# The four value products of a step, each at a place of its own

## The chip, the cores and the metric

The kernel runs on one core of one Trainium2 chip. The metric is the device time of one execution, in microseconds (us). Three executions of the kernel before took 1729.24, 1733.9 and 1734.99 us (median 1733.9). A fourth, recorded by the profiler, took 1729.78 us.

## The reference, cut to what matters

A gated cross-attention block is followed by a quantised feed-forward block. The change lies in the attention, whose values are these:

```
kv = cond @ Wkv + bkv                 # 4096 keys (4 x 1024), 512 -> 2 x 512 columns
k, v = kv[..keys], kv[..values]       # 16 heads of 32 columns each
v = fq_sym(v, axis=keys)              # 127 steps of the largest magnitude of a column over all keys
attn = softmax(fq_sym(q) @ fq_sym(k)^T)   # 2048 rows x 4096 keys, for each of 16 heads
attn = fq_unsigned(attn)              # 255 steps of a row's largest value
out = (attn @ v) @ Wp + bp
```

All four batches are one sequence here: 2048 query rows meet 4096 keys in each of the 16 heads. The values of a head group (four heads, 128 columns) need a scale over all 4096 keys before any of them can be rounded.

## The kernel before, in words

A first part (to about 240 us) projects queries and keys, stores the turned context rows `cT` in DRAM, and makes the values of head group 0. The attention then runs from about 240 to about 1465 us in 256 steps `i`, one for each head and each tile of 128 query rows. The feed-forward block follows.

The order of instructions on every engine is the order in which the program issues them (`manual_schedule`). A step of the attention has three chunks of keys (`CHUNKS`: 1536, 1536 and 1024 wide). For chunk `n`, `scores(i, n)` issues three, three or two matmuls into a PSUM tile `ps_s` (line 689), and then one VectorE instruction (line 698) which multiplies the scores by the keys' scales, writes them to the SBUF buffer `s` or `third`, and keeps the row maximum. There are two `ps_s` tiles, so that a chunk's matmuls wait until VectorE is done with the chunk two before.

After each chunk the loop runs what a plan holds for that place. `plan[i, n]` is a list of small pieces of work that are spread over the steps by hand: `plan[i, 0]` is run after chunk 0 of step `i`, `plan[i, 1]` after chunk 1, `plan[i, 2]` after chunk 2. Two kinds of work in it matter here.

The first is attention times values. `plan_values` puts a block of 32 small matmuls (`products(k)`, line 768) at place 1 of every step from step 8 on; ahead of it GpSimd casts the bytes that the block reads (line 752), one step earlier, at place 0. ScalarE's exponentials of the step before (line 718) are issued at place 0 as well.

The second is the values of head groups 1 to 3. `plan_group(g, i, 3)` is called at step 4 for group 1 and at steps 64 and 128 for groups 2 and 3. It goes through the 4096 keys in 16 pieces of 256. For piece `j`, with `u = i + 3 + 2j`, one accumulation of four float32 products (`product(j, c)`, line 616, each 128x128 by 128x256, two instructions each in the profile) is spread over the two steps `u` and `u + 1`. So the first 32 steps or so of a head group's 64 carry products, and the rest carry none. When the last product is in, ScalarE moves the result out of PSUM (`leave`, line 625), and after every second piece VectorE takes a maximum over 512 columns (`store`, line 635) in step `u + 2`. This text calls step `u + 1`, which has three of the four products in the kernel before, the late step of a piece, and step `u` the early one.

The functions that issue the pieces of a place do so in the order in which they were put into the list. `plan_group` runs once, far ahead; `plan_values` runs every four steps, for steps some five to eight ahead. A product that stands at place 1 is thus ahead of the attention block of that place, but for the first two pieces of groups 2 and 3, whose blocks are in the list already.

Of the kernel before, what the change touches and what calls it, by code (L numbers as in the profile page):

```python
# [33 lines left out]
def flamingo_kernel(  # L34
# [229 lines left out]
    def value_integers(vi, g, vt):  # L264

        nc.scalar.activation(vi, vt, AF.Identity, scale=isv[:, g : g + 1])
        return vi

    def values_by_key(vh, g, j):
        if g not in vqs:  # L270
            vqs[g] = vqp.tile([P, KT, P], F16, name="vq")
        nc.sync.dma_start_transpose(vqs[g][:, j * VB : (j + 1) * VB, :], vh)
# [24 lines left out]
    def values_weight(g):  # L297
        return wkv[:, C + g * P : C + (g + 1) * P].rearrange("(c p) n -> p c n", p=P)
# [303 lines left out]
    def plan_group(g, i, lead=1):  # L602
        wv_g = wvs.next()
        vmx = fs.tile([P, KT // VB], F32, name="vmx")
        state = {}

        def load(j):
            cT = cTs.next()
            b, a = divmod(j * VW, VB * P)
            nc.sync.dma_start(cT, cTd[b][:, :, a : a + VW])  # L610
            state["cT", j] = cT

        def product(j, c):
            if c == 0:
                state["acc"] = aav.tile([P, 512], F32, name="vacc")[:, :VW]
            nc.tensor.matmul(  # L616
                state["acc"], wv_g[:, c, :], state["cT", j][:, c, :],
                start=(c == 0), stop=(c == CC - 1),
            )

        def leave(j):
            b, a = divmod(j * VW, VB * P)
            if a == 0:
                state["v", b] = vgs.next()
            nc.scalar.activation(
                state["v", b][:, a : a + VW],
                state.pop("acc"),
                AF.Identity,
                bias=bv[:, g : g + 1],
            )  # L630
            state.pop(("cT", j))

        def store(b):
            v = state.pop(("v", b))
            nc.vector.tensor_reduce(
                vmx[:, b : b + 1], v, AX.X, ALU.max, apply_absolute_value=True
            )
            nc.sync.dma_start(vtd[g][:, b * VB * P : (b + 1) * VB * P], v)

        def fetch(j):  # L640
            vt = vgs.next()
            nc.sync.dma_start(vt, vtd[g][:, j * VB * P : (j + 1) * VB * P])
            state["vt", j] = vt

        def integer(j):
            state["vi", j] = value_integers(vis.next(), g, state.pop(("vt", j)))

        def cast(j):
            state["vh", j] = vhs.next()
            nc.vector.tensor_copy(state["vh", j], state.pop(("vi", j)))  # L650

        def turn(j):
            values_by_key(state.pop(("vh", j)), g, j)

        nc.sync.dma_start(wv_g, values_weight(g))
        load(0)
        for j in range(NV):
            u = i + lead + 2 * j
            for c, place in enumerate(((u, 2), (u + 1, 0), (u + 1, 2), (u + 1, 2))):
                plan[place].append(partial(product, j, c))  # L660
            if j + 1 < NV:
                plan[u, 1].append(partial(load, j + 1))
            plan[u + 1, 2].append(partial(leave, j))
            if (j + 1) * VW % (VB * P) == 0:
                plan[u + 2, 1].append(partial(store, j * VW // (VB * P)))
        u = i + lead + 2 * NV
        plan[u + 2, 0].append(partial(value_scale, g, vmx))
        for j in range(KT // VB):
            n = u + 3 * j
            plan[n + 1, 1].append(partial(fetch, j))  # L670
            plan[n + 3, 0].append(partial(integer, j))
            plan[n + 4, 2].append(partial(cast, j))
            plan[n + 5, 1].append(partial(turn, j))
# [754 lines left out]
    with tc.manual_schedule():  # L1428
        nc.vector.memset(less, -128.0 * INT_STEP)
        nc.vector.memset(ones_h, 1.0)  # L1430
        for i in range(len(steps)):
            h, t = steps[i]
            for n in range(len(CHUNKS)):
                scores(i, n)

                if n == 0 and t == (4 if h == 0 else 0) and h % HPG == 0 and h // HPG + 1 < NG:
                    plan_group(h // HPG + 1, i, 3)
                if n == 0 and i:
                    exps(i - 1)
                for run in plan.pop((i, n), ()):  # L1440
                    run()
            if i > 1:
                turn_exps(i - 2)
            if h + 2 < H and t % 2 == 0:
                load_piece(h + 1, t // 2)
            if 0 <= i - PAIR < TG:
                for n in ((0, 4, 2), (1, 3), (5,), (6, 7))[i - PAIR]:
                    load_piece(H - 1, n)
# [142 lines left out]
```

## Time and profile before

| what | value |
|---|---|
| three timed executions | 1729.24, 1733.9, 1734.99 us |
| the profiled execution's own time | 1729.78 us |
| its span, first to last instruction | 1728.0 us |
| mean granted clock of TensorE | 0.678 |
| VectorE busy | 1575.1 us (91%) |
| ScalarE busy | 1347.7 us (78%) |
| TensorE matmuls busy | 1291.4 us (75%) |
| GpSimd busy | 1277.7 us (74%) |

The span is the time from the first to the last instruction in the profile, and the 1.8 us between it and the execution's own time lie around it. In the profile PE is TensorE's matmuls and PEld its weight loads, DVE is VectorE, ACT is ScalarE, POOL is GpSimd. A row of a timeline gives the start, the duration, the engine, the source line, the operation, the tiles (out<-in), the shapes and the number of merged instructions; square brackets give the idle time of the engine just before it and what ended that. PEclk is the share of TensorE's full clock that was granted.

### The profile page before, as it was taken

What the parts mean: (1) busy time and instruction counts of PE and PEld (TensorE: products, weight loads), DVE (VectorE), ACT (ScalarE), POOL (GpSimd) and SP (SyncE); (2) the same over time, 40 slices, a digit from 0 to 9 for tenths busy, and PEclk for the clock granted to TensorE, in tenths of its full rate; (3) what the DMA queues carried; (4) which work ended last, traced back from release to release, by engine and by line L of the source; (5) the groups of instructions that cost most, each with busy time, mean ns of one, the idle gap of its engine ahead of it and who ended that gap; (6) DMA issues with size and microseconds to landing.
All of it is one profiled execution on the core that took longest, in us unless ns stands there. A gap on an engine that the chain in (4) does not pass through costs nothing. (4 is left out here: it accounts for less than half of the span.)

```text
span 1728.0 us, 31533 instructions
## 1 busy us (share of the span) xinstructions
PE 1291.4 (75%) x12164; PEld 589.4 (34%) x12174; DVE 1575.1 (91%) x2232; ACT 1347.7 (78%) x994; POOL 1277.7 (74%) x1276
## 2 busy tenths in 40 slices
PE   7999966888566888766687885666665576789986
PEld 3444422444222444322244432222222233434432
DVE  5786899999999999999999999999999989579996
ACT  2443467888889888889888888888887877679996
POOL 0001125888999988899988889999999998556763
PEclk9999985666555566655557655555555556889998
DMA  5876869999899999899999999999999776613424
GB/s 207 269 249 231 277 207 222 214 227 204 176 198 177 227 197 232 177 191 191 177 224 192 234 187 185 191 164 199 156 184 178 149 140 127 183 32 81 98 55 103
DMA packets 736300, 315.93 MB, mean 183 GB/s; under 512 B 658002, under 2 KB 703638, under 8 KB 729750
## 3 DMA queue, kind: packets, MB, share of 16 engines
q1 hardware_dynamic: 727094, 308.66, 82.0%
q10 hardware_dynamic: 9024, 5.24, 1.1%
q8 instruction: 95, 1.56, 0.4%
q14 instruction: 55, 0.45, 0.1%
q0 software_dynamic: 32, 0.01, 0.0%
HBM read 110.15 MB, written 40.12 MB: 87 GB/s over the span
## 5 line engine op out<-in xcount | busy, mean ns | idle before, releaser
L752 POOL CAST rT<-pT 128x2048 int16<-128x2048 uint8 x506 | 943.9, 1892 | 26.5 <-issue 6.8
L698 DVE CUSTOM_DVE_ANT_0 s<-ps_s,skb 128x1536 f32<-128x1536 f32 x531 | 806.5, 1572 | 29.0 <-PE ps_s L689 19.2
L718 ACT ACTIVATE r<-s,nb,sq 128x4096 uint8<-128x4096 f32 x177 | 673.1, 3803 | 125.8 <-POOL nb L715 106.6
L689 PE MATMUL ps_s<-kT,qT 32*128 32x512 bf16 x2048 | 437.2, 567 | 351.9 <-DVE m L698 338.4
L698 DVE CUSTOM_DVE_ANT_0 third<-ps_s,skb 128x1536 f32<-128x1536 f32 (+1 forms) x237 | 362.0, 1572 | 9.9 <-PE ps_s L689 9.3
L718 ACT ACTIVATE r<-third,nb,sq 128x4096 uint8<-128x4096 f32 x79 | 300.5, 3804 | 58.8 <-POOL nb L715 48.5
L689 PEld LDWEIGHTS <-qT 32*128 32x128 bf16 x2048 | 104.9, 98 | 638.4 <-issue 625.3
L768 PE MATMUL acc<-rT,vq 128*32 128x128 f16 x8192 | 255.2, 299 | 14.0 <-POOL rT L752 8.2
L768 PEld LDWEIGHTS <-vq 128*32 128x32 f16 x8192 | 189.4, 134 | 129.7 <-issue 108.6
L616 PE MATMUL vacc<-fx 128*128 128x256 f32 x384 | 185.3, 604 | 0.0
L713 POOL TENSOR_SCALAR m<-m 128x1 f32<-128x1 f32 x256 | 93.2, 364 | 82.4 <-DVE m L698 78.1
L454 POOL TENSOR_SCALAR nsq<-sq 128x16 f32<-128x16 f32 x16 | 3.3, 204 | 174.5 <-DVE sq L285 174.5
L417 PE MATMUL kacc<-wk_sb,cT 128*128 128x512 f32 x256 | 116.4, 598 | 0.0
L616 PEld LDWEIGHTS vacc<-fx 128*128 128x128 f32 x384 | 91.3, 277 | 58.5 <-issue 50.3
L715 POOL TENSOR_SCALAR nb<-m,nsq 128x1 f32<-128x1 f32 x256 | 66.9, 261 | 25.1
L1083 PE MATMUL ph<-fx,skb 128*128 128x512 bf16 x246 | 62.7, 398 | 1.2 <-issue 1.0
L417 PEld LDWEIGHTS kacc<-wk_sb,cT 128*128 128x128 f32 x256 | 46.7, 193 | 46.7 <-issue 45.7
L698 DVE DVE_READ_ACCUMULATOR2_ANT m<- 128x1 f32 x768 | 61.7, 80 | 0.0
L417 PE MATMUL qacc<-wq_sb,xT 128*128 128x512 f32 x128 | 57.6, 593 | 0.0
L439 DVE TENSOR_TENSOR f<-kacc,bk_sb 128x512 f32<-128x512 f32 x32 | 22.0, 689 | 34.4 <-PE kacc L417 33.3
L460 ACT COPY rows4q<-rows4q 128x1536 bf16<-128x1536 bf16 x16 | 23.5, 1471 | 27.7 <-DVE rows4q L142 27.7
L294 ACT COPY cT<-tr 128x512 f32<-128x512 f32 x32 | 18.6, 580 | 33.2 <-PE tr L293 32.9
(244 smaller groups left out, 1376.5 us busy)
## 6 DMA issues: line engine op xcount, KB each, us to landing
skb<-skd SPq DMA_DIRECT2D x32, 1024.0 KB
fx<-cTd SPq DMA_DIRECT2D x48, 512.0 KB
wt<-in_L_ffn_w_dram SPq DMA_DIRECT2D x16, 1024.0 KB
in<-in_ctx_dram SPq DMA_DIRECT2D x32, 256.0 KB
cTd<-cT SPq DMA_DIRECT2D x8, 1024.0 KB
q4d<-rows4q SPq DMA_DIRECT2D x16, 512.0 KB
vtd<-fx SPq DMA_DIRECT2D x24, 256.0 KB
fx<-vtd SPq DMA_DIRECT2D x24, 256.0 KB
```

The costliest lines, as they stand in the source:

```text
L417: nc.tensor.matmul(acc, tT[:, c, :], wk_sb[c] if kind == "k" else wq_sb[:, c, :], start=(c == 0), stop=(c == CC - 1),)
L439: nc.vector.tensor_tensor(f, acc, bk_sb, ALU.add)
L460: nc.scalar.copy(r4[:, :, 1:, :], r4[:, :, 0:1, :].to_broadcast([P, H, HPG - 1, HD]))
L616: nc.tensor.matmul(state["acc"], wv_g[:, c, :], state["cT", j][:, c, :], start=(c == 0), stop=(c == CC - 1),)
L689: nc.tensor.matmul(ps_s[:, b * KB - k0 : (b + 1) * KB - k0], qT[rows, 0, t * P : (t + 1) * P], kT[rows, 0, a * KB : (a + 1) * KB], start=True,
L698: nc.vector.tensor_tensor_reduce(s[:, k0 : k0 + w], ps_s[:, :w], skb[:, k0 : k0 + w], 1.0, -3.0e38, ALU.mult, ALU.max, m3[:, n : n + 1],)
L713: nc.gpsimd.tensor_scalar(m, m3[:, 0:1], m3[:, 1:2], m3[:, 2:3], ALU.max, ALU.max)
L715: nc.gpsimd.tensor_scalar(nb, m, nsq[:, t, h : h + 1], LN255, ALU.mult, ALU.add)
L718: nc.scalar.activation(r.rearrange("p (n two) -> p two n", two=2), s.rearrange("p (two n) -> p two n", two=2), AF.Exp, bias=nb, scale=sq[: ...
L752: cast(spreads[k][:, 2 * u : 2 * u + 2, :, :] .bitcast(I16) .rearrange("p a (two b) q -> p a two (b q)", two=2), pTs[u][:, :, k * NW : (k ...
L768: nc.tensor.matmul(acc[c * HD : (c + 1) * HD, :], vq[:, kb, h % HPG * HD : (h % HPG + 1) * HD], rT[:, c, b, :], start=(k == 0 and b == 0), ...
L1083: nc.tensor.matmul(ph[:, n, :], xqT[:, c, tok], w1T[:, c, at : at + 512], start=(c == 0), stop=False,)
```

## The change

The four products of a piece stand at the places `(u, 2)`, `(u + 1, 0)`, `(u + 1, 2)` and `(u + 1, 2)` before. After the change the third one stands at `(u + 1, 1)`, so that each place has one. Nothing else differs: the loads of `cT`, the move out of PSUM after the fourth product, the maximum and the stores keep their places.

```
             u = i + lead + 2 * j
-            for c, place in enumerate(((u, 2), (u + 1, 0), (u + 1, 2), (u + 1, 2))):
+            for c, place in enumerate(((u, 2), (u + 1, 0), (u + 1, 1), (u + 1, 2))):
                 plan[place].append(partial(product, j, c))
```

TensorE's order in a late step is then as follows; S0, S1, S2 are the score matmuls of the three chunks, c0 to c3 the products, A the attention block of 32 matmuls:

```
before: S0 c1 | S1 A     | S2 c2 c3 | S0 of the next step
after:  S0 c1 | S1 c2 A  | S2 c3    | S0 of the next step
```

In the late steps of the first two pieces of groups 2 and 3 (four of 48) the order at place 1 is A c2.

## The prediction

> **What bounds the kernel now.** I read the page's shares first, then the waits, then windows over the stretches with and without products, then one late step in the timeline. (A measurement of this kernel can tell about 0.3%, some 5.2 us, from no change.)
>
> ```profile
> PE 1291.4 (75%) x12164; PEld 589.4 (34%) x12174; DVE 1575.1 (91%) x2232; ACT 1347.7 (78%) x994; POOL 1277.7 (74%) x1276
> ```
>
> VectorE is busiest by far. The share is a mean over stages, so I asked for windows: the three stretches with products (300 to 440, 565 to 720, 870 to 1025 us) and one without (440 to 560). Columns: length, then busy time of PE, PEld, DVE, ACT, POOL with instruction counts, then the granted clock, DMA share and GB/s.
>
> ```profile
> 300.00:440.00 140.00, 114.33 (x1266) 57.37 (x1266) 133.24 (x178) 117.08 (x81) 123.50 (x115) 0.66 1.00 217
> 440.00:560.00 120.00, 73.23 (x1042) 30.78 (x1040) 119.93 (x168) 107.26 (x67) 113.61 (x105) 0.50 0.96 179
> 565.00:720.00 155.00, 132.12 (x1381) 65.52 (x1384) 146.79 (x198) 129.34 (x88) 136.58 (x126) 0.63 1.00 212
> 870.00:1025.00 155.00, 131.39 (x1405) 66.19 (x1404) 146.49 (x198) 129.37 (x89) 136.72 (x128) 0.65 0.99 209
> ```
>
> Without products VectorE is never idle (119.93 of 120) and sets the pace. With products it is idle for 6.76, 8.21 and 8.51 us: 23.5 us in all, which is what this change can win at most. The waits name who is late:
>
> ```profile
> DVE s L698 <- PE ps_s L689: 19.2, 29, 2.1
> ...
> DVE third L698 <- PE ps_s L689: 9.3, 14, 2.2
> ```
>
> That is total us, times and longest: VectorE waits for score matmuls, by some half a microsecond at a time. The timeline of step 32, a late step, shows how:
>
> ```profile
> 397.15 0.61 PE L689 MATMUL ps_s<-kT,qT 32*128 32x512 bf16 x3
> 397.60 1.22 DVE L698 CUSTOM_DVE_ANT_0 s<-ps_s,skb 128x1024 f32<-128x1024 f32 x1
> 397.69 1.22 PE L616 MATMUL vacc<-fx 128*128 128x256 f32 x2
> ...
> 398.73 1.75 DVE L698 CUSTOM_DVE_ANT_0 third<-ps_s,skb 128x1536 f32<-128x1536 f32 x1
> 398.87 0.61 PE L689 MATMUL ps_s<-kT,qT 32*128 32x512 bf16 x3
> 399.42 1.04 PE L768 MATMUL acc<-rT,vq 128*32 128x128 f16 x32
> ...
> 400.55 0.61 PE L689 MATMUL ps_s<-kT,qT 32*128 32x512 bf16 x2
> 401.09 2.08 PE L616 MATMUL vacc<-fx 128*128 128x256 f32 x4
> ...
> 402.09 1.22 DVE L698 CUSTOM_DVE_ANT_0 third<-ps_s,skb 128x1024 f32<-128x1024 f32 x1
> 403.10 1.03 PE L689 MATMUL ps_s<-kT,qT 32*128 32x512 bf16 x6
> ...
> 403.86 1.76 DVE L698 CUSTOM_DVE_ANT_0 s<-ps_s,skb 128x1536 f32<-128x1536 f32 x1 [0.54 <-PE ps_s L689]
> ```
>
> The reader is to see that TensorE has almost no idle time from 397.15 to 404.13. It waits only 0.1 us at 400.46, for chunk 0's tile. The pair c2 c3 (x4) stands ahead of the next step's S0, which comes 0.54 us late. But TensorE as a whole is late there, not the pair alone: moving a product within the step moves work within a full queue.
>
> **What the change does, part by part.** It removes no instruction and adds none. c2's operands are those of c0 and c1, which ran a step before, so it waits for nothing new. Queued behind c2 at its new place are A, S2 and c3.
>
> *The split of the pair.* A product alone takes 1.22 us (the row at 397.69), and 1.15 from its start to that of S1-type work behind it (565.89 to 567.05 in step 68). The pair takes 2.08, and 2.01 to the next start (401.09 to 403.10). Two products apart thus cost 2 x 1.15 - 2.01 = 0.29 us of TensorE more: each time the engine goes from score matmuls to a 128-row float32 product and back, a weight load stands free. What a change from a product to A costs no row shows. From below it is nothing (c2 at the pair's rate, a split for 0); from above, a whole weight load of that kind (0.29 us median by the tile's rows) on top. I take 0.29, from the nearest row, a product followed by scores.
>
> *A late step that follows a maximum (like step 32).* At half clock, from these rows: S1 starts at 398.87, c2 at 399.42 and A 1.15 later, at 400.57. A takes 0.98, so S2 starts at 401.55 (before: 400.55) and ends at 402.16. VectorE asks for it at 402.09 and waits about 0.1. c3 starts at 402.09, S0 at 403.24 instead of 403.10, and VectorE starts 0.14 us later than before. Extra: 0.15, the 0.29 less the idle 0.1 that c2 fills.
>
> *A late step that follows none (like step 68).* There c1 delays S1 already: S1 starts 567.05, A 567.59, S2 568.56 with no idle time, the pair 569.10, S0 571.11, and VectorE 571.88, which is 0.94 late. After: S2 at 569.71, done at 570.32, and VectorE, ready at 569.72, waits 0.6 for it. c3 starts at 570.25, S0 at 571.40, VectorE 0.29 later than before. Extra: the whole 0.29.
>
> *The sum.* The maximum comes after every second piece. So of 16 late steps in a group 7 are of the first kind, and 9 (the 8 odd pieces and the first) of the second: 21 x 0.15 + 27 x 0.29 = 11.0 us if the clock were always at half. The stretches' mean clock is 0.66, 0.63 and 0.65. If it is either half or full, the half share is (1 - 0.646) / 0.5 = 0.71, and at full clock neither order makes VectorE wait (there a chunk takes 0.39 and a product 0.70, rows at 415.32 and 415.64 us, clock 1.00). 11.0 x 0.71 = 7.8.
>
> *A gain in one place.* In step 8 the block A waits until 280.84 for GpSimd's cast (2.62 us), and VectorE then waits 2.24 and 1.43 us. c2 fits into that wait, and S0 comes 2.01 - 1.15 = 0.86 earlier. 7.8 - 0.9 = 6.9.
>
> *The clock.* The longer unbroken run of TensorE may earn full clock more often. The row: in 395.40 to 405.20 TensorE was busy for 9.56 of 9.80 us and the granted clock was 0.50 throughout. The Trainium skill, "TensorE: Matmul & The Clock Gate", Part 1, says that about 3.4 us of sustained activity release the throttle. By that rule nearly each late step would earn full clock, the waits would go, and the sum would be about -23 us. The window just cited speaks against counting on it: a busy run of nearly 10 us earned nothing. I give it 1 us: +6 us.
>
> *What is moved past.* A comes 1.15 us later in a late step. Its reads free an `rT` buffer for the cast of the step after next. GpSimd's casts of step 32 run 399.70 to 403.43 and use the other buffer, so over 2 us are left; without that cover each late step would cost up to 1 us of GpSimd. S2's maximum reaches GpSimd's `m` 0.1 to 0.6 later in a late step. POOL is idle 9 to 12% of these stretches, which covers it; without that it would add to the 0.1 to 0.6, not replace it. DMA places do not move.
>
> *Against the runs.* 1729.8 (profiled execution) + 6 = 1735.8. That execution is 4.1 below the median of the timed runs; the mean of all four is 1732.0. From that, 1738.
>
> **The rivals.**
>
> *No change (0.25).* c2 fills idle time before A and S2 and the clock rises a little more often: +0.15 and +0.29 shrink to nothing. For it: six of 48 late steps show no wait at all now, so the clock does rise there. Against: in step 68 there is no idle time to fill. Time 1730 to 1735.
>
> *Faster (0.16).* The pair is the culprit: with half of it ahead of A, S2 would still be in time. S2 of step 32 is ready at 401.16 and wanted at 402.09, 0.93 us of room. c2 takes 0.70 at full clock, which fits, and 1.15 at half, which doesn't. So it decides whether the clock is full while c2 runs. If half the late steps get that, half of the 23.5 us goes: 1732 - 12 = 1720; all: 1708. Against: 0.50 in the window above.
>
> *Much slower (0.07).* Products spread thinner keep the clock at half all through. The rows then give 21 x 0.69 + 27 x 1.23 = 48 us of waits in place of 23.5: about 1756. For it: a clock of 0.50 where TensorE is busy for 61% (73.23 of 120). Against: total TensorE work rises, and late steps are full in either order.
>
> **How the numbers follow.** My forecast (0.52) covers +3 to +11 us: the sum with the split between 0.15 and 0.4 us and the clock's share between none and half. 0.41 of it lies above 5.2 us, 0.11 below. Slower: 0.41 + 0.07 = 0.48. Within 0.3%: 0.25 + 0.11 = 0.36. Faster: 0.16. The range takes the forecast, the case of no change and the near third of the faster case, up to 15 above the mean of the runs: 1724 to 1747.
>
> **What would show it.** The x4 rows of L616 are gone from the late steps, and x2 rows stand at three places. VectorE's waits for `ps_s`, now 43 in 28.5 us, become 65 to 80 in 33 to 38 us: in steps like 68 one of about 0.6 before chunk 2 and one of about 0.5 before the next S0, in steps like 32 one of 0.1 and one of 0.5. VectorE's idle time in the three stretches rises from 23.5 to about 30. PE's busy time grows by some 10 us, and weight loads of `vacc` show more free time (now 50.3 us in 143). The stretch 440 to 560 keeps its pace. I am wrong if the clock in the stretches passes 0.75 (then faster), if c2 followed by A takes 0.85 instead of 1.15, or if GpSimd's casts become what the blocks wait for.

## The result, and the profile after

The changed kernel took 1747.31 us (median of five executions, 1741.87 to 1749.78), against 1733.9 before (median of five, 1729.24 to 1745.48): a ratio of 1.0075, with a 95% interval of 1.0046 to 1.0104. That is 8 to 18 us slower. The slowest execution before lies within the range of the change; the next slowest took 1734.99, and 45 further ones of the same kernel, run beside the experiments below, took 1729.85 to 1739.41. The forecast was slower, by 6; the median lies at the upper end of the range, 0.3 us above it. The profiled execution after (1749.78 us, span 1748.0) is the slowest of its five, and the one before was one of the fastest of its kernel, so the two profiles lie 20 us apart where the medians lie 13. One execution of e6 below (1845.28 us, mean clock 0.611 where its others had 0.703 to 0.710) counts as slow and is left out of its ratio.

The page's line of engine shares, after:

```profile
PE 1337.1 (76%) x12174; PEld 588.2 (34%) x12174; DVE 1579.8 (90%) x2232; ACT 1349.9 (77%) x994; POOL 1277.9 (73%) x1276
```

TensorE's busy time rose by 46 us, with the same instructions (ten matmul records of line 1083, some 2 us, are missing from the profile before). Of these, 37 us are the products' (185.3 to 222.0). The forecast had about 10 for the split of the pair, so most of the rise is something else: the same matmuls took longer. The windows, with the columns of before, show it in the clock:

```profile
300.00:440.00 140.00, 123.81 (x1196) 55.46 (x1193) 128.68 (x172) 115.25 (x77) 119.28 (x111) 0.59 0.99 212
440.00:560.00 120.00, 72.66 (x1043) 30.77 (x1040) 119.93 (x168) 106.02 (x66) 112.63 (x103) 0.50 0.95 179
565.00:720.00 155.00, 136.13 (x1325) 60.87 (x1326) 143.07 (x190) 124.89 (x83) 131.72 (x123) 0.58 0.97 208
870.00:1025.00 155.00, 136.82 (x1350) 61.12 (x1350) 144.02 (x191) 126.97 (x84) 133.90 (x125) 0.56 0.97 205
```

The stretch without products is unchanged. In the three with products VectorE is idle for 11.3, 11.9 and 11.0 us (34 in all, 23.5 before), and the granted clock has gone from 0.66, 0.63 and 0.65 to 0.59, 0.58 and 0.56. The waits (total us, times, longest) grew:

```profile
DVE s L698 <- PE ps_s L689: 25.1, 43, 2.0
...
DVE third L698 <- PE ps_s L689: 11.5, 19, 1.5
...
DVE s L698 <- ACT fx L625: 6.3, 12, 0.6
...
DVE third L698 <- ACT fx L625: 2.7, 5, 0.6
```

The first two lines are 62 waits in 36.6 us, for 43 in 28.5 before; 65 to 80 in 33 to 38 were foreseen. The view puts the other 17, in 9.0 us, down to ScalarE's move out of PSUM, and so it does with five of before, the one at the end of step 68 among them:

```profile
DVE s L698 <- ACT fx L625: 4.1, 5, 0.9
```

They end 0.58 to 0.77 us after S0's first matmul starts; the waits ahead of chunk 0 that are put down to TensorE end 0.55 to 0.77 us after it. So they are the same kind of wait, and in all there are 79 in 45.6 us, for 48 in 32.6: more on both counts than was foreseen from the 43. The timeline of step 82, a late step with no maximum ahead of it, shows the two waits of a late step:

```profile
645.34 1.22 PE L616 MATMUL vacc<-fx 128*128 128x256 f32 x2
...
645.80 1.75 DVE L698 CUSTOM_DVE_ANT_0 s<-ps_s,skb 128x1536 f32<-128x1536 f32 x1
646.49 0.61 PE L689 MATMUL ps_s<-kT,qT 32*128 32x512 bf16 x3
647.03 1.22 PE L616 MATMUL vacc<-fx 128*128 128x256 f32 x2
...
648.18 1.04 PE L768 MATMUL acc<-rT,vq 128*32 128x128 f16 x32
649.16 0.61 PE L689 MATMUL ps_s<-kT,qT 32*128 32x512 bf16 x2
...
649.70 1.22 PE L616 MATMUL vacc<-fx 128*128 128x256 f32 x2
649.81 1.23 DVE L698 CUSTOM_DVE_ANT_0 s<-ps_s,skb 128x1024 f32<-128x1024 f32 x1 [0.56 <-PE ps_s L689]
...
651.62 1.76 DVE L698 CUSTOM_DVE_ANT_0 third<-ps_s,skb 128x1536 f32<-128x1536 f32 x1 [0.58 <-PE ps_s L689]
```

The x4 row is gone; c1, c2 and c3 are three rows of 1.22. From c2's start to A's is 1.15 us (647.03 to 648.18), so the unseen change from a product to the block costs what a change from a product to scores costs. S2 is late, and the next S0 is late again.

A table of step lengths, worked out from the traces, carries the rest of this document. A length runs from the start of VectorE's chunk 0 of a step to that of the next step, averaged over the 48 late steps (21 with a maximum ahead of them, 27 without), and over the 48 early ones. "Clock" is the granted clock in the three product windows.

| kernel | late, maximum | late, none | early | clock | ratio to before, 95% |
|---|---|---|---|---|---|
| before | 5.13 | 5.17 | 4.77 | 0.66 0.63 0.65 | 1 |
| the change | 5.19 | 5.76 | 4.77 | 0.59 0.58 0.56 | 1.0046 to 1.0104 |
| e1 c1, c2 at place 0 | 4.79 | 5.24 | 4.77 | 0.68 0.63 0.59 | 0.9927 to 0.9968 |
| e2 c2, c3 at place 1 | 5.21 | 5.76 | 4.78 | 0.65 0.65 0.65 | 1.0067 to 1.0095 |
| e3 without c2 | 4.83 | 4.71 | 4.78 | 0.52 0.59 0.52 | 0.9841 to 0.9868 |
| e4 two a step, first at place 0 | 4.74 | 4.91 | 5.40 | 0.50 0.50 0.60 | 1.0060 to 1.0088 |
| e5 c2 behind the block | 5.18 | 5.55 | 4.77 | 0.53 0.58 0.60 | 1.0045 to 1.0070 |
| e6 before, with filler | 4.72 | 4.92 | 5.35 | 0.78 0.73 0.76 | 1.0057 to 1.0106 |
| e7 the change, with filler | 5.17 | 5.67 | 5.40 | 0.67 0.63 0.62 | 1.0182 to 1.0236 |
| e8 e1 with filler | 5.03 | 4.74 | 5.31 | 0.74 0.74 0.80 | 1.0039 to 1.0089 |
| e9 the change, a maximum a piece | 5.46 | 5.46 | 4.81 | 0.56 0.53 0.56 | 1.0062 to 1.0092 |
| e10 before, a maximum a piece | 5.10 | 5.13 | 4.81 | 0.66 0.62 0.61 | 0.9972 to 0.9995 |
| e11 e1, a maximum a piece | 5.12 | 4.91 | 4.81 | 0.65 0.63 0.64 | 0.9922 to 0.9958 |
| e12 two a step, first at place 1 | 4.57 | 4.86 | 5.20 | 0.63 0.61 0.63 | 0.9970 to 0.9995 |

(In e9 to e11 every late step has a maximum ahead of it; the first two columns are then the same pieces as in the others.) The first two rows settle where the time went: 21 x 0.06 + 27 x 0.59 = 17 us of the 20 between the profiles lie in the late steps, 16 of them in those with no maximum ahead. The early steps and all else kept their lengths; about 2 us arose before the first product (VectorE's first chunk starts at 242.6 us for 240.5).

A step's length mixes clocks, and what one step saves the next can lose. So a second table takes a piece's early and late step together, and only those pieces that ran at one clock throughout: the median length, with the number of pieces. Pieces up to step 12, which a long wait in step 8 disturbs, and in e6 and e7 the first pieces of groups 2 and 3, which have no filler, are left out.

| kernel | half clock: no maximum | half clock: maximum | full clock: no maximum | full clock: maximum |
|---|---|---|---|---|
| before | 10.02 (3) | 10.22 (4) | none | none |
| the change | 10.33 (10) | 10.37 (8) | 9.01 (1) | none |
| e1 | 10.03 (9) | 10.03 (6) | none | none |
| e3 | 9.18 (18) | 9.60 (14) | none | none |
| e5 | 10.33 (15) | 10.37 (12) | 9.00 (2) | none |
| e6 | 11.96 (1) | 11.96 (1) | 9.00 (3) | 9.59 (6) |
| e7 | 12.25 (6) | 11.37 (7) | 9.00 (3) | 9.59 (3) |
| e9 | 10.33 (15) | 10.33 (12) | 9.33 (2) | none |
| e10 | 10.03 (8) | 10.03 (6) | 9.33 (2) | 9.33 (2) |

At half clock the change's order costs 0.31 us a piece, or 0.15 with a maximum. At full clock its one piece took 9.01 us, twice the 4.50 that VectorE's three chunks need, so nothing waited.

### The profile page after: what moved, and what is told of

It reads as the page before. It is cut to its first block, busy times and chain, and to the rows that moved or that the text cites. A ratio compares the mean times of both kernels' runs of the same rounds, so it can differ in the third digit from the quotient of the medians.

```text
span 1748.0 us, 31543 instructions
## 1 busy us (share of the span) xinstructions
PE 1337.1 (76%) x12174; PEld 588.2 (34%) x12174; DVE 1579.8 (90%) x2232; ACT 1349.9 (77%) x994; POOL 1277.9 (73%) x1276
## 3 DMA queue, kind: packets, MB, share of 16 engines
q10 hardware_dynamic: 9024, 5.24, 1.1%
## 5 line engine op out<-in xcount | busy, mean ns | idle before, releaser
L689 PE MATMUL ps_s<-kT,qT 32*128 32x512 bf16 x2048 | 446.2, 579 | 328.1 <-DVE m L698 317.8
L689 PEld LDWEIGHTS <-qT 32*128 32x128 bf16 x2048 | 100.5, 99 | 629.9 <-issue 614.7
L616 PE MATMUL vacc<-fx 128*128 128x256 f32 x384 | 222.0, 679 | 0.1
L460 ACT COPY rows4q<-rows4q 128x1536 bf16<-128x1536 bf16 x16 | 23.5, 1471 | 27.1 <-DVE rows4q L142 26.9
```

Source lines behind the costliest of these rows:

```text
L460: nc.scalar.copy(r4[:, :, 1:, :], r4[:, :, 0:1, :].to_broadcast([P, H, HPG - 1, HD]))
L616: nc.tensor.matmul(state["acc"], wv_g[:, c, :], state["cT", j][:, c, :], start=(c == 0), stop=(c == CC - 1),)
L689: nc.tensor.matmul(ps_s[:, b * KB - k0 : (b + 1) * KB - k0], qT[rows, 0, t * P : (t + 1) * P], kT[rows, 0, a * KB : (a + 1) * KB], start=True,
```

## The experiments

**e1: c1 and c2 together, both at place 0.**

```
+            for c, place in enumerate(((u, 2), (u + 1, 0), (u + 1, 0), (u + 1, 2))):
```

> c1 and c2 together at place 0 of the late step, c3 alone at place 2: c2 leaves place 2 as in the change, but next to c1, so that no further switch between score matmuls and products arises (three groups of products a piece, as before). Theory of the full queue and its switches: at half clock steps like 32 give S0 0.18 us earlier than before and steps like 68 the same, so about 3 us faster than before (-5 to 0), and VectorE's idle time in the product stretches stays at 20 to 25 us. Rival, c2's leaving place 2 delays the next chunk wherever it goes: S1 now comes 0.5 us late in steps like 68, and the kernel is as slow as the changed one (+10 to +16).

Measured: 0.9948, that is 6 to 13 us faster than before, with 18.6 us of VectorE's idle time in the three stretches. The direction is that of the theory; the size is beyond its upper end. Taking c2 from place 2 is thus no loss in itself, and can be a gain. The timeline of step 72 shows why:

```profile
587.40 2.07 PE L616 MATMUL vacc<-fx 128*128 128x256 f32 x4
...
589.41 0.61 PE L689 MATMUL ps_s<-kT,qT 32*128 32x512 bf16 x3
...
590.12 1.75 DVE L698 CUSTOM_DVE_ANT_0 s<-ps_s,skb 128x1536 f32<-128x1536 f32 x1
...
593.38 1.76 DVE L698 CUSTOM_DVE_ANT_0 s<-ps_s,skb 128x1536 f32<-128x1536 f32 x1 [0.35 <-PE ps_s L689]
```

Behind a maximum TensorE starts S0 early, the pair fits in ahead of S1, which is ready at 590.02 (589.41 + 0.61) for 590.12, and c3 alone leaves less to wait for at the step's end.

**e2: c2 and c3 together, both at place 1.**

```
+            for c, place in enumerate(((u, 2), (u + 1, 0), (u + 1, 1), (u + 1, 1))):
```

> c2 and c3 together, both at place 1 ahead of the attention block. Number of switches as before. If the number of switches alone counts: as before, within 3 us. If the place counts, by the rows of before at half clock: in steps like 32 S2 starts at 402.41 instead of 400.55, VectorE waits 0.97 before it and starts the next step 0.43 later than before; in steps like 68 0.58 later. 21 x 0.43 + 27 x 0.58 = 25 us at half clock throughout, 17 with the clock of before: slower than before by 15 to 25 us, with nearly all of VectorE's waits ahead of chunk 2.

Measured: 1.0081, 12 to 16 us slower. That is at or below the lower end of what was expected. There is no switch more than before, and yet the kernel is as slow as the change: the number of switches alone is not what counts. The waits are those of the rows, and they stand ahead of chunk 2 (45 us in the 48 late steps, and none ahead of the next S0):

```profile
DVE s L698 <- PE ps_s L689: 34.1, 38, 2.1
DVE third L698 <- PE ps_s L689: 16.4, 17, 1.4
```

**e3: without c2.**

```
+                if c == 2:
+                    continue
```

> Leaves out the third of the four products of groups 1 to 3, so the values of those groups lack a quarter of their sum; all else as before. It gives the time without the moved product. By the rows at half clock a step like 32 then has no wait and a step like 68 one of 0.07: about 22 us faster than before (-18 to -24), whatever the clock is. The moved product would then have cost about 22 us at its old place (0.46 a piece) and 35 at its new one (0.73 a piece). If instead something other than TensorE's queue makes the late steps late, less than half of the 22 us comes off.

Measured: 0.9855, 23 to 28 us faster than before, a little more than expected. VectorE's idle time in the three stretches falls from 23.5 to 7.9 us, at a clock of only 0.52 to 0.59. So most of what VectorE waits for there is the fourth product in the late step's queue. A moved product costs 25 / 48 = 0.52 us at its old place and, with the 13 of the change, 0.79 at its new one.

**e4 and e12: four products alone, two a step.** The two kernels differ in the first product's place.

```
e4  +            for c, place in enumerate(((u, 0), (u, 2), (u + 1, 0), (u + 1, 2))):
e12 +            for c, place in enumerate(((u, 1), (u, 2), (u + 1, 0), (u + 1, 2))):
```

> The four products stand alone, as in the change, but two a step: places (u, 0), (u, 2), (u + 1, 0), (u + 1, 2). As many switches as the change, but the early step takes two products and none stands ahead of the attention block. If the sum over the two steps counts, 0.29 us more than before: slower than before by 5 to 14 us. If the late step's queue counts: at half clock a step has 4.9 us of TensorE work against 4.57 of VectorE's own and 0.17 of maxima, so about 0.16 x 96 = 15 us of waits in place of 23.5 (a loss of 0.3 in some steps where c0 waits for ScalarE's move out of PSUM): faster than before by 5 to 15 us.

Measured, e4: 1.0074, 10 to 15 us slower. The late steps did become short (4.74 and 4.91), but the early ones went from 4.77 to 5.40. The waits of the weight loads tell why:

```profile
PEld vacc L616 <- ACT fx L625: 44.8, 45, 3.4
```

c0 at place 0 asks for the accumulator that ScalarE is still moving out, 1 us a piece. I had put this at 0.3.

> Four products alone, two a step, with the first at place 1 of the early step instead of place 0, where it waited for ScalarE's move out of PSUM (45 us in 45 waits). Sum of TensorE work as in the change. If that wait is what spoiled the other variant: the early step's length falls from 5.40 us to 5.0 to 5.2, the late steps stay below 5.0, and the kernel is within -5 to +8 us of before. If the four single products themselves (a queue of 9.8 us at half clock per two steps) are too much: +8 to +14, as the change.

Measured, e12: 0.9983, 1 to 5 us faster than before, with the early step at 5.20, the upper end of what was expected. The same line:

```profile
PEld vacc L616 <- ACT fx L625: 22.7, 40, 3.1
```

Half of that wait is gone, and 16 us of the kernel's time with the new place. The clocks differ too (0.50 to 0.60 in e4, 0.61 to 0.63 in e12), so that not all of the 16 need be the wait. e12 has the change's number of products alone, with the same four switches, and is 15 us faster than it. So single products are affordable where two steps share them; three of them and the block in one step, as in the change and in e5, were not.

**e5: c2 behind the block.** The loop runs a list for half a place further, and c2 stands there.

```
-            for c, place in enumerate(((u, 2), (u + 1, 0), (u + 1, 1), (u + 1, 2))):
+            for c, place in enumerate(((u, 2), (u + 1, 0), (u + 1, 1.5), (u + 1, 2))):
...
-                for run in plan.pop((i, n), ()):
+                for run in plan.pop((i, n), []) + plan.pop((i, n + 0.5), []):
```

> As the change, but c2 is issued behind the attention block of place 1 in every late step, directly ahead of chunk 2, instead of ahead of the block. Groups of products and sum of TensorE work as in the change. Theory of the full queue: S2 waits for c2 in either order, so the time is that of the changed kernel (+10 to +16 against before), with the same waits before chunk 2. Rival, c2 ahead of the block harms by delaying the block: back to within 5 us of before.

Measured: 1.0057, 8 to 12 us slower than before; the interval overlaps that of the change. Delaying the attention block is not the harm. Late steps without a maximum are 5.55 for 5.76, but at half clock throughout a piece takes what it takes in the change (10.33 and 10.37 us). So the two orders cost the same at one clock, and the shorter mean goes with pieces at a higher clock.

**e6, e7, e8: filler for the clock.** Six small matmuls in each early step but a group's first, at places 0 and 1, in before, in the change, and in e1. They write unused columns of the accumulator's bank (the line that keeps that tile in `state` is left out here):

```
+        def filler(h):
+            for _ in range(3):
+                nc.tensor.matmul(
+                    state["tile"][:, VW:], ident_b, heads[h][0][:, 0, :VW],
+                    start=True, stop=True,
+                )
...
+            if j:
+                for n in range(2):
+                    plan[u, n].append(partial(filler, steps[u][0]))
```

> The kernel before, with two times three small bf16 matmuls (128x128 by 128x256) added at places 0 and 1 of each early step, into unused columns of the accumulator's bank; they add TensorE activity where the early step has room. Theory that the granted clock sets the waits: if the activity holds the clock up (stretches above 0.85), the waits for ps_s in the late steps go, and the kernel is 10 to 23 us faster than before although TensorE does more. If the clock stays near 0.65, the added work (some 0.6 to 0.9 us at each place at half clock) makes early steps late too: 10 to 40 us slower.

> The changed kernel with the same added matmuls. Theory that the change's loss beyond the split of the pair is a lower clock: if the clock is held up (above 0.85), its late steps have no waits either, and it is within 4 us of the kernel before with the same added matmuls. Rival, the order within the late step harms by itself: it stays 10 us or more behind that one. If the clock isn't held up: slower than the change by 10 to 40 us.

> The faster variant with c1 and c2 at place 0, with the same added matmuls. If the clock is held up: as the two others with them, 10 to 23 us faster than before. If not: slower than without them by 10 to 40 us.

Measured: 1.0081, 1.0209 and 1.0064. None held the clock above 0.85, so none is the clean test that was meant. The window lines of e6 and of e7 from 565 to 720 us:

```profile
565.00:720.00 155.00, 128.61 (x1432) 62.01 (x1435) 143.37 (x192) 124.62 (x84) 132.46 (x123) 0.73 1.02 208
```

```profile
565.00:720.00 155.00, 134.59 (x1341) 59.66 (x1338) 139.22 (x185) 122.31 (x82) 128.74 (x118) 0.63 0.96 204
```

Part of the reading stands all the same. In e6 the clock rose to 0.73 and more, and the late steps came down from 5.13 and 5.17 to 4.72 and 4.92. What was won there went into the early steps (5.35), where the filler waits for the same move out of PSUM as c0 in e4 (37.8 us in 37 waits):

```profile
PE vacc L624 <- ACT fx L633: 37.8, 37, 2.0
```

In e7 the same filler brought the clock only to 0.62 to 0.67, and the late steps stayed long. It is 22 us behind e6, which is the outcome I had written for "the order harms by itself". But its clock was lower too, so the two totals don't part the causes. The second table does. At full clock throughout a piece takes 9.00 us, or 9.59 with a maximum, in e6 and in e7 alike: there the change's order costs nothing. At half clock, with the filler, a piece without a maximum takes 11.96 in e6 (one piece) and 12.25 in e7, again 0.3 apart, but one with a maximum 11.96 (one piece) and 11.37. So the order by itself is no harm at full clock, and e7 had less of that than e6. Why it had less is not shown.

**e9, e10, e11: a maximum after every piece.** VectorE reduces 256 columns a piece instead of 512 every second piece, in the change, in before, and in e1 (`store` and the size of `vmx` change with it, which is left out here):

```
-            if (j + 1) * VW % (VB * P) == 0:
-                plan[u + 2, 1].append(partial(store, j * VW // (VB * P)))
+            plan[u + 2, 1].append(partial(store, j))
```

> The changed kernel, with VectorE's maximum taken over 256 columns after every piece instead of over 512 after every second. VectorE then stands still for the product queue before every late step (some 0.42 us, from 0.68 for 512 columns with 0.53 of them streaming) instead of before every second one; it costs VectorE 0.16 x 24 = 4 us. Theory that the loss lies in the late steps without a maximum ahead of them (length 5.76 us against 5.19 for the others): the two kinds become alike, about 5.3 to 5.4, and the kernel is about 5 us faster than the change, +4 to +11 against before. Rival, the order alone harms, whatever stands before the step: slower than the change by the 4 us of VectorE.

> The kernel before with the same maxima after every piece. Its two kinds of late steps are alike already (5.13 and 5.17 us), because the clock is up in many of those without a maximum. So there is little to gain and the 4 us of VectorE to pay: within 4 us of before, rather slower (0 to +4).

> The faster variant (c1 and c2 at place 0) with the same maxima. Its late steps without a maximum are 5.24 us, the others 4.79; if the former come down to about 4.85, 27 x 0.39 = 10 us less the 4 us of VectorE: 5 us faster than that variant, 12 to 16 faster than before. If the clock falls with it, no gain.

Measured: 1.0077, 0.9983 and 0.9940. In e9 the two kinds of late steps did become alike, at 5.46, a little over what was expected, but their mean was 5.51 already. So the gain of 5 us did not come, and the kernel is as slow as the change. That corrects the theory that the loss belongs to steps without a maximum: it shows there, but it is TensorE's queue over the pair of steps that is too long. At half clock a piece's two steps take 10.33 us in e9, with or without a maximum ahead, and 10.33 and 10.37 in the change; in the order of before with the same maxima (e10), and in e1, they take 10.03. Room given to one step is taken from the other. The waits of e9 are more and shorter than those of the change:

```profile
DVE s L699 <- PE ps_s L690: 27.6, 60, 2.1
...
DVE third L699 <- PE ps_s L690: 11.7, 26, 1.5
```

e10 came out 1 to 5 us faster than before, where I had expected the same or slower. e11 (1725.63 us median) is, with e1 (1726.87 in its own comparison), the fastest kernel here that computes the reference; their intervals overlap.

## Why the prediction was right in its direction and short in its size

**The split of the pair, 0.29 us at half clock: held.** In the change a late step without a maximum is 5.82 us at half clock (step 82: 645.80 to 651.62), and 5.52 in the kernel before (step 68: 566.36 to 571.88): 0.30. With a maximum it is 5.27 for 5.13, which is 0.14, where 0.15 was worked out. The two waits of step 82 are 0.56 and 0.58, where 0.6 and 0.5 were worked out.

**The sum "11.0 x 0.71", and the 1 us taken off for the clock: failed.** The multiplication let the added work shrink with the share of half clock, but kept the clock itself as before. The split came in whole: 26 x 0.30 + 21 x 0.14 = 10.7 us (step 8 apart), about the 11.0 without its factor. The term to add was what the old waits cost when the clock leaves them. Before, late steps without a maximum, step 8 left out, averaged 5.04 us, 0.48 below their own half-clock length, because the clock was up in the late step or in the early one ahead of it in many. In the change they average 5.72, 0.10 below theirs. So of their 0.68 us, 0.30 is the split and 0.38 the clock. Those with a maximum grew by 0.06 only, 0.08 less than the split alone. Over all 48 late steps of the two profiles, 17.4 us are 10.7 for the split, -1.6 for step 8 and 8 for the rest, most of it the clock (some 0.7 are steps 10 and 12, behind step 8). The forecast had 7.8, -0.9 and -1.

The 8 us hold for these two profiles, which had clocks of 0.678 and 0.654. Over the five executions of the change the clock was 0.652 to 0.662, over the 45 of before that ran beside the experiments 0.657 to 0.678. The medians are 13 us apart and not 20, so between usual executions the clock's part is smaller; no run gives it.

The clock's timing within the step supports this. In the traces the mean granted clock over chunks 0, 1 and 2 of an early step and then of a late one is 0.66, 0.77, 0.69 and 0.55, 0.56, 0.59 before; after the change it is 0.70, 0.65, 0.52 and 0.52, 0.51, 0.56. Full clock now comes just behind the late step and is gone when c1 of the next piece runs: c1 had it in 16 of the 48 pieces before and in 2 after. The runs of the unchanged kernel lean the same way: of the eleven beside e5 to e8 the two fastest (1731.8 and 1732.2 us) had a mean clock of 0.678 and 0.676, the two slowest (1735.8 and 1735.9) 0.668 and 0.670. Time and clock go together with a correlation of -0.94 in those, of -0.74 in the 23 beside e9 to e12, and of only -0.46 in the eleven beside e1 to e4. Both are observations; no experiment here set the clock alone.

**The credit to a longer unbroken run: wrong sign.** The doubt about it was right. e4 shows it further, by its window:

```profile
565.00:720.00 155.00, 147.52 (x1326) 62.49 (x1323) 144.92 (x194) 126.41 (x84) 133.43 (x122) 0.50 0.99 208
```

TensorE is busy for 95% of 155 us, and the granted clock is half throughout. The Trainium skill, "TensorE: Matmul & The Clock Gate", Part 1, has the throttle released by about 3.4 us of sustained activity; by the busy time that the profile gives, this window does not show it.

**The gain in step 8: more than foreseen.** Its two waits were 2.24 and 1.43 us and are 1.52 and 0.58: 1.6 us less, for the 0.9 of the forecast.

**What is moved past: held.** e5 puts the block back in its place and gains little, and GpSimd's and ScalarE's busy times are nearly unchanged (1277.7 to 1277.9 and 1347.7 to 1349.9 us). GpSimd was idle for 12% of each of the three stretches before, not for 9 to 12.

**The rivals.** The faster one needed room for c2 ahead of S2, and at half clock there is none, as its condition said; c2 had full clock in 2 of the 48 pieces. "Much slower" came in part: its condition was that the clock falls, which it did in half the amount. I had given that 0.07.

What stays open is why the clock falls. Without filler, kernels with a pair had 0.59 to 0.68 in these windows, most of those with single products 0.50 to 0.60; but e12, all singles, had 0.61 to 0.63. Neither TensorE's busy share nor the number of pairs orders them. The last section has what the traces add to this.

## What to carry to other kernels

When the work of an engine that runs in order is spread by hand, count what fits between two points where the next engine takes something from it, at the slowest clock that the profile shows there. Here one place holds one product, and only the place with room ahead of S1 holds a pair; moving a piece from a full place to another in the same full step gains nothing, and cutting a back-to-back pair adds a weight load that stands free (0.3 us at half clock; at full clock, where VectorE set the pace, it cost nothing). And a term that is priced "at half clock, times the share of half clock" needs a second line for what the change does to that share.

## What the runs showed of the hardware

The granted clock did not follow TensorE's busy time: it was 0.50 with TensorE busy for 73.23 of 120 us (before, without products), 0.78 in e6 with 114.87 of 140, and 0.50 in e4 with 147.52 of 155. And with a change of order within one step, and the same instructions, the mean clock of a whole execution was 0.654 for 0.678 (the two profiled executions), and TensorE's busy time was 46 us longer, the split of the pairs included.

The traces show one thing more. In the two profiles every change of the granted clock (79 before, 61 after) lies within 0.006 us of a grid of 3.413 us. Three such periods are 10.24 us, close to the 10.02 to 10.37 us that a piece's two steps take at half clock, so that the grid's points move only slowly through the steps. Within the pieces the clock rose 29 times before, at many places of the two steps, and 20 times after, always 4.66 to 5.34 us behind the start of a late step's chunk 0. That a small change in a piece's length moves the clock by way of these places is a guess that fits; no run tests it.
